# Reordering the start-up tiles of a cross-attention and spectral-FFN kernel: transposes, evictions and norms trade places in five tiles

## The chip, the cores and the metric

The kernel runs on one core of one Trainium2 chip. A core has a matrix engine (TensorE, "PE" in the profile, with weight loads shown apart as "PEld"), a vector engine (VectorE, "DVE"), an activation engine (ScalarE, "ACT"), a general engine (GpSimd, "POOL") and a queue that issues DMAs (SyncE, "SP"). Each engine works through its own list of instructions in order. The metric is device time in microseconds, the median of several runs; lower is better.

## What is computed

Everything is float32. `x` is (2, 2048, 512), the context is (2, 128, 512), 16 heads of 32.

```python
def attention(x, enc, mask):            # x already layer-normed
    q, k, v = x @ wq + bq, enc @ wk + bk, enc @ wv + bv      # split into 16 heads
    score = (q @ k.T) / sqrt(32) * mask
    score = where(score == 0, -1e9, score)
    return softmax(score) @ v @ wo + bo

def ffn(x):                             # x already layer-normed
    y_freq = fft(x) @ (w_real + 1j * w_imag)
    return real(ifft(y_freq)) + bias

x = x + attention(layernorm(x), ctx, mask)
x = x + ffn(layernorm(x))
```

The FFN is linear, so the kernel folds both transforms and the complex weight into one real 512 x 512 matrix, `m_ffn`, computed once on the chip.

## The kernel before

**Tiling.** The 4096 rows are taken in 8 groups of 512 rows (`i`), each of 4 row tiles of 128 (`t`). A tile is written here as (group, row tile). A group goes through these stages: its rows less their first element (`relative`, on POOL for most groups), row statistics on DVE, `query_norm` on DVE, `query_transposes` (four 128x128 transposes on PE and a copy by ACT into `xnT`), four query chains `q[0]` to `q[3]` (PE, evicted by ACT with the bias), then for each row tile scores and softmax, the transposes of the weights, `context`, the output projection `o[t]`, a second layer norm, and the FFN chain `y`.

**One tile of the softmax.** `begin(i, t)` issues 32 score matmuls into two PSUM tiles, a half of 8 heads each. For each half: `masked` (DVE, L345, PSUM to SBUF), `maxima` (DVE: L352 over the whole half, the reduction L354, and the tiny L355), `exponentials` (ACT: eight L361 activations, each with a read of its accumulator), `divided` (a reciprocal on DVE, L373, and the product on POOL, L374). Then `transposed_weights(i, t, first, end, eng)`: for each of four head sets, four transposes on PE (L391) into a PSUM bank and a copy out by ACT (L398), or by DVE (L396) where `nc.vector` is given. Both halves must have been divided before any of it.

**Buffers.** PSUM has two buffers of each kind: `sc` for scores (two banks each), `tp` for transposes, `mm` for chains. The third user of a `tp` or `mm` buffer waits until the copy or eviction of the first is done. In SBUF, `rel` has 4 buffers, `xnT` and `cT` one, `w` (a half of the weights) five.

**What runs beside the first tiles.** In tiles (0,1) to (1,1) the start-up work is woven in: the second value chain `values[1]`; the matrix `m_ffn`, made from four `First` products `h[0]` to `h[3]` (PE, evicted by ACT; `first()` is four small POOL operations, L676 and L678; `second()` two DVE operations, L689 and L690) and four `Mirrored` products `m[0]` to `m[3]` (PE, evicted by two ACT operations, L731 and L737, then two POOL operations, L738 and L739); the queries of groups 1 and 2; the statistics and norms of groups 2 and 3. Each `Mirrored` product reads all four halves that `second()` finishes. `load_first_rows` sends four small DMAs on SP's queue that read the result of `h[2]`.

**Order.** The order of instructions is written out by hand: every engine runs its share of the calls in the order in which the Python code makes them, and semaphores are set from the buffers read and written. For (0,0) to (1,0) the calls stand one by one; from (1,1) on a helper, `slot(...)`, issues a tile from lists of work. Its argument `soon=True`, used for (1,1), puts the exponentials ahead of the first chain's eviction, and the second half's exponentials ahead of the second pair of weight transposes.

The few lines that show what a chain with work in between does:

```python
for c in range(NC):
    nc.tensor.matmul(ps, lhs(c), rhs(c), start=(c == 0), stop=(c == NC - 1))
    if c == HC - 1:
        call(between)
```

Of the kernel before, what the change touches and what calls it, by code (L numbers as in the profile page):

```python
# [22 lines left out]
def kernel(  # L23
# [34 lines left out]
    nc = tc.nc  # L58
# [5 lines left out]
    NC = D // P  # L64
    NR = P // DH
    HH = H // 2
    TG = 4
# [6 lines left out]
    work = ctx.enter_context(tc.tile_pool(name="work", bufs=2))  # L74
# [11 lines left out]
    HC = NC // 2  # L86
# [36 lines left out]
    def load_residual(i):  # L123
        b, q0 = place(i)
        xs = groups[i] = big_tile("x", 2, f"x_{i}")
        for t in range(TG):
            nc.sync.dma_start(xs[:, t, :], x[b, q0 + t * P : q0 + (t + 1) * P, :])
# [146 lines left out]
    def query_norm(i, t):  # L274
        mv, rstd = stats[i]
        normalize(rels[i][t], rels[i][t], mv[:, t, :], rstd[:, t : t + 1])

    def query_transposes(i, t):
        if t == 0:
            xnTs[i] = big_tile("xnT", 1, f"xnT_{i}")  # L280
        transpose_rows(
            xnTs[i][:, :, t * P : (t + 1) * P], rels[i][t], f"a{i}_{t}", nc.scalar
        )

    class Queries:
# [5 lines left out]
        def pe(self):  # L291
            i, g = self.i, self.g
            if i not in qTs:
                qTs[i] = big_tile("qT", 2, f"qT_{i}")
            self.ps = chain(
                f"q_{i}_{g}",
                lambda c: wq[:, c, g * P : (g + 1) * P],
                lambda c: xnTs[i][:, c, self.first * P :],
                width=GQ - self.first * P,
                spare=self.spare,  # L300
            )
# [78 lines left out]
    def transposed_weights(i, t, first, end, eng=None, banks=None):  # L380
        if t == 0 and first == 0:
            pts[i] = [big_tile("pt", 6, f"pt_{i}_{g}") for g in range(NC)]
        ws = weights[i, t]
        for g in range(first, end):
            ps = (
                banks[g]
                if banks
                else ps_tp.tile([P, NR, P], FP, tag="tp", name=f"tpw_{i}_{t}_{g}")
            )
            for r in range(NR):  # L390
                nc.tensor.transpose(  # L391
                    ps[:, r, :], ws[r // 2].w[:, (r % 2) * NC + g, :], ident
                )
            dst = pts[i][g][:, :, t * P : (t + 1) * P]
            if eng:
                eng.tensor_copy(dst, ps)  # L396
            else:
                nc.scalar.copy(dst, ps)  # L398
# [4 lines left out]
    def context(i, first, end, eng=nc.scalar):  # L403

        b = place(i)[0]
        if first == 0:
            cTs[i] = big_tile("cT", 1, f"cT_{i}")
        cT = cTs[i]
        for g in range(first, end):
            ps = ps_mm.tile([P, GQ], FP, tag="mm", name=f"c_{i}_{g}")  # L410
            for r in range(NR):
                h = g * NR + r
                nc.tensor.matmul(  # L413
                    ps[r * DH : (r + 1) * DH, :],
                    v[:, b, h * DH : (h + 1) * DH],
                    pts[i][g][:, r, :],
                    start=True,
                    stop=True,
                )
            if eng is nc.scalar:  # L420
                nc.scalar.copy(cT[:, g, :], ps)
            else:
                eng.tensor_copy(cT[:, g, :], ps)

    def output_bias(i):

        xs = groups[i]
        for t in range(TG):
            nc.gpsimd.tensor_tensor(xs[:, t, :], xs[:, t, :], bo, ALU.add)  # L429
# [153 lines left out]
    class Values:  # L583
        def __init__(self, b):
            self.b = b

        def pe(self):
            self.ps = chain(
                f"v_{self.b}",
                lambda c: encT[:, c, self.b * K : (self.b + 1) * K],  # L590
                lambda c: wv[:, c, :],
            )

        def evict(self):
# [148 lines left out]
    def run(job):  # L743
        job.pe()
        job.evict()

    def begin(i, t):
        sc = scores(i, t)
        weights[i, t] = [Softmax(i, t, hf, sc[hf]) for hf in range(2)]
        return weights[i, t]  # L750
# [110 lines left out]
    h = [First(what, g) for what in range(2) for g in range(HC)]  # L861
    m = [Mirrored(f"m_{g}", half_of(g), m_ffn[:, g, :]) for g in range(NC)]
    rest = [Queries(0, g, 1, g >= HC) for g in range(NC)]
    q = [Queries(1, g) for g in range(NC)]
    values = [Values(b) for b in range(B)]

    w = begin(0, 0)
# [21 lines left out]

    w = begin(0, 1)  # L890
    w[0].masked()
    for t in range(TG):
        query_transposes(1, t)
        relative(2, t, nc.gpsimd)
    w[0].maxima()
    values[1].pe()
    w[0].exponentials()
    w[1].masked()
    values[1].evict()
# [3 lines left out]
    w[1].exponentials()  # L903
    h[0].evict()
    w[0].divided()
    transposed_weights(0, 0, HC, NC, nc.vector)
    query_statistics(2, 0, TG)
    run(q[0])
    w[1].divided()
    h[0].first()  # L910

    load_rows(3)
    w = begin(0, 2)
    w[0].masked()
    q[1].pe()
    w[0].maxima()
    w[0].exponentials()
    w[1].masked()
    q[1].evict()
    transposed_weights(0, 1, 0, HC, nc.vector)  # L920
    w[1].maxima()
    run(q[2])
# [2 lines left out]
    for t in range(TG):  # L925
        query_norm(2, t)
    w[0].divided()
    h[0].second()
    run(q[3])
    w[1].divided()  # L930

    q = [Queries(2, g) for g in range(NC)]
    w = begin(0, 3)
    w[0].masked()
    h[1].pe()
    h[1].evict()
    h[1].first()
    w[0].maxima()
    h[2].pe()
    h[2].evict()  # L940
    h[2].first()
    w[0].exponentials()
    w[1].masked()
    transposed_weights(0, 2, 0, HC, nc.vector)
    h[1].second()
    h[3].pe()
    h[3].evict()
    h[3].first()
    for t in range(TG):
        query_transposes(2, t)  # L950
    w[1].maxima()
    w[0].divided()
    relative(3, 0, nc.gpsimd)
# [2 lines left out]
    load_residual(0)  # L956
    rows_m = load_first_rows("rows_m", [x.lhs(HC)[0:1, :] for x in m])
    w[1].exponentials()
    transposed_weights(0, 2, HC, NC, nc.vector)
    run(q[0])  # L960
    w[1].divided()
    relative(3, 1, nc.gpsimd)

# [1 line left out]
    w = begin(1, 0)  # L965
    w[0].masked()
    m[0].pe()
    add = first_rows("add_m", rows_m)
# [2 lines left out]
    relative(3, 2, nc.gpsimd)  # L971
    relative(3, 3, nc.gpsimd)
    m[1].pe()
    w[0].exponentials()
    w[1].masked()
    transposed_weights(0, 3, 0, HC, nc.vector)
    w[1].maxima()
    w[0].divided()
    m[1].evict(add[:, 1:2])
    m[2].pe()  # L980
    m[2].evict(add[:, 2:3])
    transposed_weights(0, 3, HC, NC)
# [5 lines left out]
    w[1].divided()  # L988
    query_statistics(3, 2, TG)

    def last_of_m():
        m[3].pe()
        m[3].evict(add[:, 3:4])


    for i in range(1, last - 1):
        p, pp, n, nn = i - 1, i - 2, i + 1, i + 2
        q = [Queries(n, g) for g in range(NC)]
        q_nn = Queries(nn, 0)
        o = [Project(p, t) for t in range(TG)]  # L1000
        f_p = Ffn(p, 0)
        second = [q[2], q[3], None]
        if i > 1:
            f_pp = [Ffn(pp, t) for t in range(TG)]
            second = [q[2], q[3], f_pp[3]]

        def if_pp(*work):
            return list(work) if i > 1 else []

        if i > 1:  # L1010
            load_rows(nn)
            load_mask(n)
            load_residual(p)
            slot(
                i,
                0,
                [f_pp[1], f_pp[2], q[1]],
                turned=(p, TG - 1),
                early=[(ffn_transposes, pp, 2)],
                pool=[(relative, nn, t, nc.gpsimd) for t in range(TG)],  # L1020
                on_b=[(ffn_norm, pp, 3), (query_statistics, nn, 0, 2)],
                on_c=[(query_statistics, nn, 2, TG)],
                end=[(context, p, 0, 2)],
            )
        slot(
            i,
            1,
            second,
            turned=(i, 0),
            soon=(i == 1),  # L1030
            early=[
                (context, p, 2, NC),
                (ffn_transposes, pp, 3) if i > 1 else (last_of_m,),
            ],
            pool=[(output_bias, p)],
            on_b=[(query_norm, nn, 0), (query_norm, nn, 1)],
        )
        slot(
            i,
            2,  # L1040
            o[:3],
            turned=(i, 1),
            early=[(query_transposes, nn, 0), (query_transposes, nn, 1)],
            on_a=[(ffn_statistics, p, 0)],
            on_b=[(ffn_norm, p, 0), (query_norm, nn, 2), (query_norm, nn, 3)],
            on_c=[(ffn_statistics, p, 1)],
            end=[(ffn_transposes, p, 0)],
        )
        slot(
            i,  # L1050
            3,
            [o[3], f_p, q_nn],
            turned=(i, 2),
            early=[(query_transposes, nn, 2), (query_transposes, nn, 3)],
            on_a=[(ffn_statistics, p, 2)],
            on_b=[(ffn_norm, p, 1), (ffn_statistics, p, 3)],
            on_c=[(ffn_norm, p, 2)],
            end=[(ffn_transposes, p, 1)],
        )
# [4 lines left out]
    i, n, p, pp = last - 1, last, last - 2, last - 3  # L1064
    load_mask(n)
    load_residual(p)
    q = [Queries(n, g) for g in range(NC)]
# [7 lines left out]
        turned=(p, TG - 1),  # L1075
# [184 lines left out]
```

## Time and profile before

| | us |
|---|---|
| median of 3 runs | 539.77 (538.93 to 540.01) |
| profiled execution | 538.45 |
| its span, first to last instruction | 536.4 |
| PE busy in the span | 524.0 |
| DVE busy | 446.2 |
| ACT busy | 336.4 |
| POOL busy | 336.8 |

PE works at its full granted clock throughout. The span is the time from the first to the last instruction on the core; 2.05 us of the execution lie around it. Busy shares are averages over the whole span; the tiles that the change touches lie between about 36 and 111 us. The scores of the tiles begin on PE at these times:

| tile | (0,1) | (0,2) | (0,3) | (1,0) | (1,1) | (1,2) | (1,3) |
|---|---|---|---|---|---|---|---|
| scores start, us | 35.95 | 50.68 | 64.95 | 81.34 | 96.64 | 110.14 | 127.22 |

### The profile page before, as it was taken

What the parts mean: (1) busy time and instruction counts of PE and PEld (TensorE: products, weight loads), DVE (VectorE), ACT (ScalarE), POOL (GpSimd) and SP (SyncE); (2) the same over time, 40 slices, a digit from 0 to 9 for tenths busy, and PEclk for the clock granted to TensorE, in tenths of its full rate; (3) what the DMA queues carried; (4) which work ended last, traced back from release to release, by engine and by line L of the source; (5) the groups of instructions that cost most, each with busy time, mean ns of one, the idle gap of its engine ahead of it and who ended that gap; (6) DMA issues with size and microseconds to landing.
All of it is one profiled execution on the core that took longest, in us unless ns stands there. A gap on an engine that the chain in (4) does not pass through costs nothing.

```text
span 536.4 us, 8808 instructions
## 1 busy us (share of the span) xinstructions
PE 524.0 (98%) x3028; PEld 293.8 (55%) x3028; DVE 446.2 (83%) x623; ACT 336.4 (63%) x1284; POOL 336.8 (63%) x276
## 2 busy tenths in 40 slices
PE   8999989989999999999999999999999999999997
PEld 7755576445545555455545555455545555455444
DVE  4789999899887998879987999879967899899351
ACT  3376676566687666666777666666777676766210
POOL 2769487935795449825795459925755466856450
PEclk9999999999999999999999999999999999999999
DMA  9962020000510006000510005000310201301102
GB/s 318 384 221 78 1 81 20 1 1 0 185 53 2 20 24 208 7 20 1 186 51 0 21 14 203 20 21 0 117 43 25 75 0 60 100 0 41 39 0 79
DMA packets 22892, 36.49 MB, mean 68 GB/s; under 512 B 2104, under 2 KB 7488, under 8 KB 22848
## 3 DMA queue, kind: packets, MB, share of 16 engines
q1 hardware_dynamic: 22160, 34.75, 18.8%
q10 hardware_dynamic: 688, 1.18, 0.6%
q8 instruction: 24, 0.39, 0.3%
q14 instruction: 20, 0.16, 0.1%
HBM read 27.53 MB, written 8.39 MB: 67 GB/s over the span
## 4 chain that ended last, share of the span: by engine, by line
PE 73%; DVE 19%; ACT 6%; DMA 1%; issue 1%; SPq 0%; ACTq 0%; DVEq 0%
PE y L210 16%; PE o L210 16%; PE q L210 15%; PE tpw L391 7%; PE c L413 5%; PE sc L326 5%; ACT w L361 5%; DVE w L352 5%; DVE nmax L354 4%; DVE w L345 4%; PE tp_a L194 2%; PE tp_f L194 2%; PE k L558 1%; DVE nmax L355 1%; DVE norm_f L227 1%; DMA enc<-in_ctx_dram 1%
## 5 line engine op out<-in xcount | busy, mean ns | idle before, releaser
L361 ACT ACTIVATE w<-w,nmax 128x128 f32<-128x128 f32 x512 | 198.3, 395 | 26.7 <-DVE nmax L355 26.0
L374 POOL TENSOR_TENSOR w<-w,rden 128x1024 f32<-128x1024 f32 x62 | 118.2, 1907 | 79.8 <-DVE rden L373 62.2
L210 PE MATMUL o<-wo,cT 128*128 128x512 f32 x256 | 115.3, 594 | 0.0
L210 PE MATMUL q<-xnT,wq 128*128 128x512 f32 (+1 forms) x256 | 111.8, 581 | 1.5 <-ACT odd_m L737 0.9
L210 PE MATMUL y<-m_ffn,nT 128*128 128x512 f32 x248 | 112.1, 594 | 0.5 <-DVE x L514 0.5
L361 ACT ACTIVATION_READ_ACCUMULATOR w<-w,nmax 128x1 f32 x512 | 99.3, 194 | 0.0
L398 ACT COPY pt<-tpw 128x512 f32<-128x512 f32 x110 | 58.8, 586 | 56.8 <-PE tpw L391 56.6
L352 DVE SCALAR_TENSOR_TENSOR w<-w 128x1024 f32<-128x1024 f32 x64 | 89.9, 1405 | 0.8
L345 DVE TENSOR_TENSOR w<-sc,mask 128x1024 f32<-128x1024 f32 x64 | 77.4, 1211 | 13.2 <-PE sc L326 12.5
L354 DVE TENSOR_REDUCE nmax<-w 128x8 f32<-128x1024 f32 x64 | 78.1, 1220 | 2.2
L391 PEld LDWEIGHTS tpw<-ident,w 128*128 128x128 f32 x496 | 57.5, 141 | 31.9 <-issue 28.3
L210 PEld LDWEIGHTS o<-wo,cT 128*128 128x128 f32 x256 | 46.2, 190 | 47.5 <-issue 46.1
L210 PEld LDWEIGHTS q<-xnT,wq 128*128 128x128 f32 x256 | 46.4, 190 | 46.6 <-issue 40.2
L210 PEld LDWEIGHTS y<-m_ffn,nT 128*128 128x128 f32 x248 | 44.5, 190 | 45.2 <-issue 44.2
L391 PE MATMUL tpw<-ident,w 128*128 128x128 f32 x496 | 65.2, 274 | 0.8 <-ACT pt L398 0.4
L469 POOL TENSOR_TENSOR x<-x,bf 128x512 f32<-128x512 f32 x32 | 50.4, 1576 | 19.1 <-DVE norm_f L227 19.1
L223 POOL TENSOR_SCALAR rstd_f<-mv_f 128x1 f32<-128x1 f32 x32 | 17.9, 558 | 65.3 <-DVE mv_f L220 65.3
L429 POOL TENSOR_TENSOR x<-x,bo 128x512 f32<-128x512 f32 x32 | 48.1, 1532 | 0.0
L244 POOL TENSOR_SCALAR rel<-rows 128x512 f32<-128x512 f32 x26 | 43.6, 1689 | 1.6 <-PE tp_a L194 1.6
L326 PEld LDWEIGHTS sc<-kT,qT 32*128 32x128 f32 x1024 | 31.4, 186 | 15.3 <-issue 13.6
L196 ACT COPY nT<-tp_f 128x512 f32<-128x512 f32 x29 | 16.9, 583 | 34.1 <-PE tp_f L194 34.0
L373 DVE RECIPROCAL rden<-den 128x8 f32<-128x8 f32 x64 | 12.6, 197 | 30.9 <-ACT w L361 30.8
(92 smaller groups left out, 566.1 us busy)
## 6 DMA issues: line engine op xcount, KB each, us to landing
rows<-in_x_dram SPq DMA_DIRECT2D x32, 256.0 KB, 4.2
x<-in_x_dram SPq DMA_DIRECT2D x32, 256.0 KB, 4.5
out_dram<-x SPq DMA_DIRECT2D x31, 256.0 KB, 2.0
mask<-in_mask_Bx1xSxS_fk_dram SPq DMA_DIRECT2D x8, 256.0 KB, 4.7
wk<-in_L_xattn_wk_w_dram ACTq DMA_DIRECT2D x2, 512.0 KB, 7.0
wq<-in_L_xattn_wq_w_dram SPq DMA_DIRECT2D x1, 1024.0 KB, 6.8
wr<-n_L_ffn_w_freq_real_dram SPq DMA_DIRECT2D x2, 512.0 KB
wi<-n_L_ffn_w_freq_imag_dram SPq DMA_DIRECT2D x2, 512.0 KB, 8.2
```

What stands on the lines that cost most here:

```text
L210: nc.tensor.matmul(ps, lhs(c), rhs(c), start=(c == 0), stop=(c == NC - 1))
L244: eng.tensor_scalar(d, xt, xt[:, 0:1], None, ALU.subtract)
L326: nc.tensor.matmul(sc[r // 2][:, r % 2, g, :], qTs[i][rows, g, t * P : (t + 1) * P], kT[rows, g, b * K : (b + 1) * K], start=True, stop=True,)
L345: nc.vector.tensor_tensor(self.w, self.sc.rearrange("p r g k -> p (r g) k"), self.mrow, ALU.mult)
L352: nc.vector.scalar_tensor_tensor(w, w, 0.0, w, ALU.is_equal, ALU.subtract)
L354: nc.vector.tensor_reduce(self.nmax, w, AX.X, ALU.min)
L361: nc.scalar.activation(w[:, h, :], w[:, h, :], AF.Exp, bias=self.nmax[:, h : h + 1], scale=-UNIT, accum_out=self.den[:, h : h + 1],)
L374: eng.tensor_tensor(w, w, rden.unsqueeze(2).to_broadcast([P, HH, K]), ALU.mult)
L391: nc.tensor.transpose(ps[:, r, :], ws[r // 2].w[:, (r % 2) * NC + g, :], ident)
L398: nc.scalar.copy(dst, ps)
L429: nc.gpsimd.tensor_tensor(xs[:, t, :], xs[:, t, :], bo, ALU.add)
L469: nc.gpsimd.tensor_tensor(xt, xt, bf, ALU.add)
```

## The change

Nothing is added or taken out of the computation; calls trade places, and one group of copies changes its engine.

- Tile (0,1): two of the four transposes of group 1's rows stay behind the scores; the other two go into the middle of the second value chain. The chain `q[0]` goes ahead of the second pair of weight transposes, whose copies move from DVE to ACT.
- Tile (0,2): `q[1]` is evicted ahead of the exponentials; `h[0].second()` moves out to the next tile.
- Tile (0,3): the transposes of group 2's rows go right behind the scores, two ahead of `h[1]` and two behind it; `h[2]` and `h[3]` go behind the first exponentials; `h[0].second()` comes in; `q[0]` goes ahead of the second pair of weight transposes.
- Tile (1,0): `m[1]` is evicted ahead of the exponentials.
- Tile (1,1) is written out rather than issued by `slot`: the second pair of weight transposes, with its copies, goes ahead of the second half's exponentials; two norms of group 3 go ahead of the division of the first half; `output_bias` goes behind `m[3]`'s eviction.

```diff
-        def pe(self):
+        def pe(self, between=()):
             self.ps = chain(
                 f"v_{self.b}",
                 lambda c: encT[:, c, self.b * K : (self.b + 1) * K],
                 lambda c: wv[:, c, :],
+                between=between,
             )
...
 
     w = begin(0, 1)
     w[0].masked()
+    query_transposes(1, 0)
+    query_transposes(1, 1)
     for t in range(TG):
-        query_transposes(1, t)
         relative(2, t, nc.gpsimd)
     w[0].maxima()
-    values[1].pe()
+    values[1].pe(between=[(query_transposes, 1, 2), (query_transposes, 1, 3)])
     w[0].exponentials()
     w[1].masked()
     values[1].evict()
...
     w[1].exponentials()
     h[0].evict()
     w[0].divided()
-    transposed_weights(0, 0, HC, NC, nc.vector)
+    q[0].pe()
+    transposed_weights(0, 0, HC, NC)
+    q[0].evict()
     query_statistics(2, 0, TG)
-    run(q[0])
     w[1].divided()
     h[0].first()
 
     load_rows(3)
     w = begin(0, 2)
     w[0].masked()
-    q[1].pe()
+    run(q[1])
     w[0].maxima()
     w[0].exponentials()
     w[1].masked()
-    q[1].evict()
     transposed_weights(0, 1, 0, HC, nc.vector)
     w[1].maxima()
     run(q[2])
...
     for t in range(TG):
         query_norm(2, t)
     w[0].divided()
-    h[0].second()
     run(q[3])
     w[1].divided()
 
     q = [Queries(2, g) for g in range(NC)]
     w = begin(0, 3)
     w[0].masked()
+    query_transposes(2, 0)
+    query_transposes(2, 1)
     h[1].pe()
+    query_transposes(2, 2)
+    query_transposes(2, 3)
     h[1].evict()
+    w[0].maxima()
+    h[0].second()
     h[1].first()
-    w[0].maxima()
-    h[2].pe()
-    h[2].evict()
-    h[2].first()
     w[0].exponentials()
     w[1].masked()
     transposed_weights(0, 2, 0, HC, nc.vector)
     h[1].second()
+    h[2].pe()
+    h[2].evict()
+    h[2].first()
     h[3].pe()
     h[3].evict()
     h[3].first()
-    for t in range(TG):
-        query_transposes(2, t)
     w[1].maxima()
     w[0].divided()
     relative(3, 0, nc.gpsimd)
...
     load_residual(0)
     rows_m = load_first_rows("rows_m", [x.lhs(HC)[0:1, :] for x in m])
     w[1].exponentials()
+    run(q[0])
     transposed_weights(0, 2, HC, NC, nc.vector)
-    run(q[0])
     w[1].divided()
     relative(3, 1, nc.gpsimd)
 
...
     relative(3, 2, nc.gpsimd)
     relative(3, 3, nc.gpsimd)
     m[1].pe()
+    m[1].evict(add[:, 1:2])
     w[0].exponentials()
     w[1].masked()
     transposed_weights(0, 3, 0, HC, nc.vector)
     w[1].maxima()
     w[0].divided()
-    m[1].evict(add[:, 1:2])
     m[2].pe()
     m[2].evict(add[:, 2:3])
     transposed_weights(0, 3, HC, NC)
...
     w[1].divided()
     query_statistics(3, 2, TG)
 
-    def last_of_m():
-        m[3].pe()
-        m[3].evict(add[:, 3:4])
+    w = begin(1, 1)
+    w[0].masked()
+    context(0, 2, NC)
+    m[3].pe()
+    m[3].evict(add[:, 3:4])
+    output_bias(0)
+    w[0].maxima()
+    q[2].pe()
+    w[0].exponentials()
+    w[1].masked()
+    q[2].evict()
+    transposed_weights(1, 0, 0, HC, nc.vector)
+    w[1].maxima()
+    run(q[3])
+    transposed_weights(1, 0, HC, NC)
+    w[1].exponentials()
+    query_norm(3, 0)
+    query_norm(3, 1)
+    w[0].divided()
+    w[1].divided()
 
 
     for i in range(1, last - 1):
...
         q_nn = Queries(nn, 0)
         o = [Project(p, t) for t in range(TG)]
         f_p = Ffn(p, 0)
-        second = [q[2], q[3], None]
-        if i > 1:
-            f_pp = [Ffn(pp, t) for t in range(TG)]
-            second = [q[2], q[3], f_pp[3]]
-
-        def if_pp(*work):
-            return list(work) if i > 1 else []
-
         if i > 1:
             load_rows(nn)
             load_mask(n)
             load_residual(p)
+            f_pp = [Ffn(pp, t) for t in range(TG)]
             slot(
                 i,
                 0,
...
                 on_c=[(query_statistics, nn, 2, TG)],
                 end=[(context, p, 0, 2)],
             )
-        slot(
-            i,
-            1,
-            second,
-            turned=(i, 0),
-            soon=(i == 1),
-            early=[
-                (context, p, 2, NC),
-                (ffn_transposes, pp, 3) if i > 1 else (last_of_m,),
-            ],
-            pool=[(output_bias, p)],
-            on_b=[(query_norm, nn, 0), (query_norm, nn, 1)],
-        )
+            slot(
+                i,
+                1,
+                [q[2], q[3], f_pp[3]],
+                turned=(i, 0),
+                early=[(context, p, 2, NC), (ffn_transposes, pp, 3)],
+                pool=[(output_bias, p)],
+                on_b=[(query_norm, nn, 0), (query_norm, nn, 1)],
+            )
         slot(
             i,
             2,
```

## The prediction

> **What bounds the kernel now.** I read the page first: the engine shares, then windows of TensorE (PE), then PE's waits, then the chain of waits, and last the timeline of VectorE (DVE) and GpSimd (POOL) where two operations stretch each other.
>
> ```profile
> PE 524.0 (98%) x3028; PEld 293.8 (55%) x3028; DVE 446.2 (83%) x623; ACT 336.4 (63%) x1284; POOL 336.8 (63%) x276
> ```
>
> PE carries the span, so a reordering can only win where PE stands still. The windows (start:end, length, PE busy) say where that is:
>
> ```profile
> 36.00:113.70 77.70, 71.56 (x507) 1.00 0.10 32
> 113.70:128.30 14.60, 14.60 (x84) 1.00 0.00 1
> 128.30:142.90 14.60, 14.60 (x88) 1.00 0.23 69
> ```
>
> From 36 to 113.7 us, the very tiles that are edited, PE is idle for 77.70 - 71.56 = 6.1 us; after that it is full. The waits of PE up to 120 us (total, times, longest):
>
> ```profile
> PE tp_a L194 <- ACT pt L398: 2.3, 1, 2.3
> PE tp_a L194 <- ACT xnT L196: 1.7, 3, 1.2
> ...
> PE q L210 <- ACT odd_m L737: 0.9, 1, 0.9
> PE q L210 <- ACT qT L307: 0.7, 1, 0.7
> PE tpw L391 <- ACT pt L398: 0.4, 1, 0.4
> ```
>
> All end on a copy or eviction by ScalarE (ACT). Why ACT is late is in the chain of waits:
>
> ```profile
> 87.24 3.19 ACT w L361 x16
> 90.43 0.36 ACT m_ffn L731
> 90.79 0.26 ACT odd_m L737
> 91.06 0.04 issue
> 91.10 3.70 PE q L210 x8
> ...
> 111.41 1.73 ACT w L361 x9
> 113.14 0.48 ACT pt L398
> 113.61 0.04 issue
> 113.66 1.14 PE tp_a L194 x8
> ```
>
> PE's next work needs a PSUM buffer whose copy is queued behind eight exponentials. But between such places the same chain runs through DVE (masked product, L352, L354) for most of 36 to 91 us: PE's gaps are partly the echo of a slow DVE, and this decides how much of the 6.1 us comes back. DVE itself is slowed by POOL, as the timeline shows:
>
> ```profile
> 52.92 1.90 POOL L374 TENSOR_TENSOR w<-w,rden 128x1024 f32<-128x1024 f32 x1
> 53.15 2.75 DVE L352 SCALAR_TENSOR_TENSOR w<-w 128x1024 f32<-128x1024 f32 x1
> ...
> 77.16 1.90 POOL L374 TENSOR_TENSOR w<-w,rden 128x1024 f32<-128x1024 f32 x1 [0.27 <-DVE rden L373]
> 77.22 2.12 DVE L690 TENSOR_TENSOR half<-u_half 128x254 f32<-128x254 f32 x1
> ```
>
> L352 takes 1.22 us alone and 2.75 beside a division; L690 0.4 alone and 2.12.
>
> **What the Trainium skill says.** "SBUF — State Buffer", section "Who interferes with whom": DVE and GpSimd share one port pair under an exclusive lock; a DVE operation with two SBUF inputs, or a tensor_scalar in a 2-port mode, and a GpSimd operation shut each other out for the whole instruction, whoever starts first. The trace agrees: L352 ended 1.1 us after the division's end (55.90 against 54.82); copies out of PSUM and the reductions (1.22 us throughout) aren't touched. "Perfetto Trace Analysis", section "Identifying the Most-Contended Engine", warns that matmul busy time is a poor measure of distance to the peak. I use it only to find idle PE, where it serves: the gaps have named waits.
>
> **The change part by part.** I follow PE, ACT, DVE and POOL by hand with the durations of the timeline: scores 1.10, two sets of transposes 0.87, a chain 3.44, a First 1.95, a Mirrored 1.93 (PE, start to start); masked product 1.25, L352 1.22, L354 1.25, two PSUM copies 1.27, a norm 0.45 (DVE); eight exponentials 3.1, an eviction 0.68, two copies 1.05 (ACT); a division 1.90 (POOL). A tile is (group, row tile).
>
> S1, tile (0,1). Before, transposes and value chain take PE from 37.05 to 42.86 = 5.81. With two transposes inside the chain it is 0.87 + 3.44 + 0.87 = 5.2. With q[0] put before the second pair of weight transposes their 0.4 wait is covered: 42.2 + 0.87 + 1.95 + 3.44 + 0.87 gives scores of (0,2) at 49.4 (was 50.68). DVE loses two copies to ACT, 1.27, but the fourth row statistic now waits for POOL's relative at 49.8; the masked product of (0,2) starts at 50.8 (was 51.89). POOL's relatives need the two later transposes read first; these are done by 40.5, before subtract_columns frees POOL at 42.5: nothing.
>
> S2, tile (0,2). The weight transposes of (0,1) need its second division, and POOL is full from 39.42 to 54.8 (subtract, relatives, division, rstd), so that doesn't move, 54.8 to 55.2: PE, early at 53.95, idles 1.25 and q[2] starts at 56.1 as before (56.20). The early part is given back here. Then q[1] evicted ahead of the exponentials removes 0.7 to 0.8 before q[3]; scores of (0,3) at 64.0 (was 64.95). h[0].second leaves DVE's queue between norms and second reciprocal, where the division stretched it to 2.4: the masked product of (0,3) starts at 65.1 (was 66.61).
>
> S3, tile (0,3). Transposes behind the scores and around h[1] take out PE waits of 1.2 + 0.2 + 0.2 and the gap before them; scores of (1,0) could start at 79.0 (was 81.34). Against it, ACT's new order is xnT copies, h[1].evict, exponentials (70.0, was 71.31), and only then h[2].evict (73.1, was 70.21) and h[3].evict (73.7, was 74.40). POOL's h[2].first waits for L352's port until 74.4; h[2].first and h[3].first take 1.65 each, and with h[2].second between them h[3].first ends at 78.2 (was 76.89). Then h[3].second on DVE and the first division on POOL both want the port. No row of before shows who wins from this start. DVE first: h[3].second ends at 79.1. POOL first: 78.2 + 1.9 + 0.8 to 1.1 = 81.2; was 80.41. m[0] reads every half row and waits for it, and two DVE copies, the reciprocal and the masked product of (1,0) stand behind: that product at 80.4 or 82.5 (was 82.55). I take the middle and keep both ends. The row loads on SP's queue stand behind h[2].second (77.6, was 79.34), not behind h[3].
>
> S4, tile (1,0). m[1].evict ahead of the exponentials frees the buffer for q[1]: the 0.9 wait goes. Exponentials start between 84.9 and 87.3 (was 87.24), q[1] between 88.5 and 90.2 (was 91.10), scores of (1,1) between 93.8 and 95.6 (was 96.64): 1.0 to 2.8 gained, middle 1.9. On POOL the two m[1] operations (1.5) go ahead of a division whose reader runs after 102 us: hidden by about 6 us.
>
> S5, tile (1,1) and the next. Copies ahead of the second exponentials take away the 2.3 wait of tp_a, and norms ahead of the division cost 0.9 in place of 2.53. PE's scores of (1,2) come at 110.14 - 1.9 = 108.2 and the transposes follow with no wait. But the second exponentials now wait for the last weight copy: they start 1.05 later relative to PE, at 109.1 (was 109.96), end at 112.2, and behind their reciprocal stands the masked product of (1,2): 112.35 (was 113.29), 0.95 earlier only. The division ends at 114.2, and PE, with o[0] done at 113.2, waits 1.0 for it; then norm_f of (0,0), 125.6 before, ends at 124.65, and PE, there at 122.85, waits 1.8. So 126.69 becomes 124.65: 2.0. The 2.3 is mostly replaced by waits on DVE's chain. output_bias behind m[3] on POOL ends near 107, read at 118: nothing; with that cover gone it would cost its 1.5.
>
> **Sum.** After 128 us PE was full, and the work is the same, so 2.0 stays: span 536.4 - 2.0 = 534.4, execution 538.45 - 2.0 = 536.4. The median of the runs, 539.77, stands 1.3 above the profiled execution; I take the difference over to it: 537.8.
>
> **Rivals.** 0.2% of 539.77 is 1.08 us; below that this measurement can't tell a change.
> (a) The forecast: waits of ACT go, DVE's chain takes their place, 1.1 to 2.9 gained, 537.8. Chance 0.45.
> (b) DVE wins the port in S3 and the stretched L352 shrink as well: PE recovers 3 to 4.5 of its 6.1, about 536.2. For it: h[0].second, norms and two copies leave DVE, 1.7 + 1.6 + 1.3 = 4.6 of its time. Against it: POOL's queue is full to 54.8 and again near 80 to 99. Chance 0.23.
> (c) The waits come back entirely: POOL wins in S3 and the 1.05 of S5 counts in full: 0 to 1 gained, 539.3. Chance 0.20.
> (d) Slower: POOL becomes the bound in tile (0,3). If h[2].first and h[3].first, now behind the exponentials, end 1 us later than my 78.2, and L689 loses the port to the division and L690 to the relative (1.6 more), h[3].second ends at 83.8; every us beyond 81.2 takes one from the 1.1 of its end: -1.5, 541.3. It decides from h[3].second ending at 82.3 (slower at all) or 83.4 (measurably). Chance 0.12.
>
> **Range.** 535.6 to 540.1: (a) and (c) whole and half of (b). Faster by over 0.2% 0.68, within 0.2% 0.20, slower 0.12.
>
> **What would show it.** Right: the 2.3, 0.9 and 0.7 waits are gone; tp_a of group 3 follows the scores of (1,2) directly; new PE waits on POOL w L374 and on norm_f appear near 54, 113 and 123; the h[3].second pair ends between 79 and 81.3; PE's scores of (1,3) start near 125.2 (was 127.22). Wrong: no new PE wait at tiles (0,2) and (1,2), or idle PE of over 6 us before 127. The forecast falls if h[3].second ends after 82, or if PE's windows after 128 are no longer full.

## The result and the profile after

| | before | changed |
|---|---|---|
| median, us | 539.89 (4 runs) | 535.32 (4 runs: 534.98 to 536.54) |
| ratio, 95% interval | | 0.9922 (0.9901 to 0.9943) |
| profiled execution, us | 538.45 | 534.98 |
| its span, us | 536.4 | 533.0 |
| the same on another chip, median, us | 538.18 (11 runs) | 534.63 (6 runs) |
| ratio there, 95% interval | | 0.9943 (0.9928 to 0.9958) |

By the medians the change makes the kernel faster by 0.6 to 0.8%; the profiled executions differ by 3.5 us and their spans by 3.4. The kernel before takes one of two values some 1.6 us apart, 536.4 to 537.0 or 537.9 to 539.9 on the later chips: all 37 executions of the lower kind had a granted clock of at least 0.999, but 30 of the 45 of the upper kind had one of 0.996 or 0.997, so that in these the clock may be the cause (0.3% of the 524.0 us that PE is busy would be 1.6 us, by estimate). The profiled execution shown ahead of the prediction is one of the upper kind, at full clock; the last section comes back to it. Between the lower values of the two kernels on the second chip, 536.8 to 536.9 and 534.2 to 534.7, the gain is 2.2 us, or 0.4%.

In the changed kernel the new code shifts later lines by one (L657 becomes L658, L690 and L691 are the two operations of `second()`). The windows of PE that answer to those shown of before (start:end, length, PE busy, instructions, granted clock, DMA share, GB/s):

```profile
36.00:113.70 77.70, 75.06 (x526) 1.00 0.10 32
113.70:128.30 14.60, 12.93 (x76) 1.00 0.00 1
128.30:142.90 14.60, 14.60 (x82) 1.00 0.42 134
```

Up to 113.7 us PE is idle for 2.6 us in place of 6.1; but the next window, full before, now has a gap of 1.7. The waits of PE from 0 to 120 us, and those after 120 us:

```profile
PE tpw L391 <- DVE pt L396: 1.4, 1, 1.4
...
PE tpw L391 <- POOL w L374: 0.9, 2, 0.5
PE tpw L391 <- ACT xnT L196: 0.3, 1, 0.3
...
PE tp_a L194 <- ACT xnT L196: 0.2, 1, 0.2
```

```profile
PE tp_f L194 <- DVE norm_f L227: 1.9, 2, 1.7
```

The 2.3, 1.7, 0.9 and 0.7 us on ACT are gone or down to 0.5 together. In their place stand waits on DVE and POOL: copies in (1,0), the divisions of (0,1) and (1,1), and `norm_f` in (1,2).

Starts of the score matmuls on PE show where the 3.4 us came from. The third row is a second profile of the kernel before, of its lower value (536.88 us, span 534.9), the fourth one of the changed kernel on that chip (span 532.5).

| tile | (0,1) | (0,2) | (0,3) | (1,0) | (1,1) | (1,2) | (1,3) | (0,1) to (1,3) |
|---|---|---|---|---|---|---|---|---|
| before | 35.95 | 50.68 | 64.95 | 81.34 | 96.64 | 110.14 | 127.22 | 91.27 |
| changed | 35.58 | 49.09 | 63.14 | 77.49 | 93.19 | 106.70 | 123.84 | 88.26 |
| before, again | 35.05 | 49.12 | 63.40 | 79.85 | 95.15 | 108.65 | 125.72 | 90.67 |
| changed, again | 35.07 | 48.58 | 62.62 | 76.98 | 92.68 | 106.19 | 123.33 | 88.26 |

I call the last column the stretch; it is the measure of the experiments, since it leaves out most of the start-up's DMAs. It is read from one profile of each kernel; the changed kernel gave 88.26 on both chips. Between the two first rows it shrinks by 3.01; 0.37 more lie ahead of (0,1), before any edit. Of the 3.01, 1.83 are idle time of PE (6.14 us of the stretch before, 4.31 after). The other 1.18 are busy time, 85.13 and 83.95 us for the same 559 instructions: not all of the gain stood in the profile as a wait. After (1,3) nothing differs: 536.4 - 127.22 = 409.18 and 533.0 - 123.84 = 409.16. Between the last two rows it shrinks by 2.41, tile by tile: 0.56 in (0,1), 0.24 in (0,2), 2.09 in (0,3), then -0.40, -0.01 and -0.07. Tile (1,1), with the largest wait of the kernel before, gives nothing in the end. That asked for experiments.

### The profile page after: what moved, and what is told of

Read it like the earlier page. It is cut to its first block, busy times and chain, and to the rows that moved or that the text cites. A ratio compares the mean times of both kernels' runs of the same rounds, so it can differ in the third digit from the quotient of the medians.

```text
span 533.0 us, 8813 instructions
## 1 busy us (share of the span) xinstructions
PE 522.4 (98%) x3028; PEld 293.3 (55%) x3028; DVE 440.6 (83%) x621; ACT 337.5 (63%) x1286; POOL 336.8 (63%) x276
## 3 DMA queue, kind: packets, MB, share of 16 engines
q10 hardware_dynamic: 688, 1.18, 0.6%
## 4 chain that ended last, share of the span: by engine, by line
PE 74%; DVE 17%; ACT 4%; issue 2%; POOL 1%; DMA 1%; SPq 0%; ACTq 0%; POOLq 0%; DVEq 0%
PE y L210 16%; PE q L210 16%; PE o L210 14%; PE tpw L391 7%; PE c L413 5%; PE sc L326 5%; DVE w L352 4%; ACT w L361 3%; DVE nmax L354 3%; DVE w L345 3%; PE tp_f L194 2%; PE tp_a L194 2%; PE k L558 1%; DVE norm_f L227 1%; PE v L210 1%
## 5 line engine op out<-in xcount | busy, mean ns | idle before, releaser
L374 POOL TENSOR_TENSOR w<-w,rden 128x1024 f32<-128x1024 f32 x62 | 119.3, 1924 | 74.1 <-DVE rden L373 56.6
L352 DVE SCALAR_TENSOR_TENSOR w<-w 128x1024 f32<-128x1024 f32 x64 | 88.1, 1377 | 0.8
L244 POOL TENSOR_SCALAR rel<-rows 128x512 f32<-128x512 f32 x26 | 44.7, 1731 | 1.3 <-PE tp_a L194 1.3
```

The costliest lines, as they stand in the source:

```text
L244: eng.tensor_scalar(d, xt, xt[:, 0:1], None, ALU.subtract)
L352: nc.vector.scalar_tensor_tensor(w, w, 0.0, w, ALU.is_equal, ALU.subtract)
L374: eng.tensor_tensor(w, w, rden.unsqueeze(2).to_broadcast([P, HH, K]), ALU.mult)
```

## The experiments

Theory T is that of the prediction: DVE's chain, slowed by POOL on their shared port, sets PE's pace, and a wait of PE on ACT is worth only what DVE leaves of it. Rival R: each wait on ACT that goes is worth its length. All times below stand beside the kernel before on the same chip, whose median was 536.95 for the first four experiments, 538.26 for the next four and 538.18 for the last. Medians of the kernel before move with the mix of its two values, so I judge by the stretch and give the times beside it.

**Tile (1,1) alone, both ways.** First the changed kernel with its (1,1) in the old order:

```diff
     w[0].masked()
+    output_bias(0)
     context(0, 2, NC)
...
-    output_bias(0)
...
     run(q[3])
-    transposed_weights(1, 0, HC, NC)
     w[1].exponentials()
+    transposed_weights(1, 0, HC, NC)
+    w[0].divided()
     query_norm(3, 0)
     query_norm(3, 1)
-    w[0].divided()
     w[1].divided()
```

> The changed kernel with tile (1,1) in its old order. Measure: the stretch on PE from the first score matmul of (0,1) to that of (1,3), 91.27 us before, 88.26 changed. Theory T (PE's gaps after the edit are set by DVE's chain): the 2.3 us wait of tp_a on ACT's copies comes back, and the new waits on norm_f (1.67) and on the division (0.44) vanish for it; stretch 88.3, within 0.6, time within 0.1% of the changed kernel. Rival R (each wait on ACT is worth its length): stretch 90.6, time 2.3 us above the changed kernel.

Measured: stretch 88.18, against 88.26; median 534.62 us, ratio to before 0.9946 (0.993 to 0.9963). Then the kernel before with the new (1,1) alone (the same lines, the other way):

> The kernel before with tile (1,1) alone in the new order. T: the 2.3 us wait of tp_a goes and is replaced by waits on norm_f and on the division; stretch 91.3, within 0.6, time within 0.1% of before. R: stretch 89.0, time 2.3 us below before.

Measured: stretch 90.71, against 90.67; median 537.03 us, ratio 0.999 (0.9979 to 1.0001). The waits of PE from 100 to 127 us, of the changed kernel with the old (1,1) and then of the kernel before with the new one:

```profile
PE tp_a L194 <- ACT pt L398: 2.3, 1, 2.3
```

```profile
PE tp_f L194 <- DVE norm_f L227: 1.7, 1, 1.7
PE tpw L391 <- POOL w L374: 0.4, 1, 0.4
```

The two are exchanged for each other to within 0.2 us. R is out for the largest of the waits: its 2.3 us were worth nothing here. The chain of waits of the changed kernel has the way from one to the other:

```profile
106.98 0.60 ACT pt L398
107.59 3.08 ACT w L361 x16
110.67 0.02 issue
110.69 0.20 DVE rden L373
110.89 1.10 DVE w L345
111.99 0.02 issue
112.02 2.01 DVE w L352
...
121.37 1.77 DVE norm_f L227
123.14 0.14 issue
123.28 0.63 PE tp_f L194 x4
```

The copies ahead of the exponentials free PE's buffer and delay the exponentials; the reciprocal waits for them, and the masked product of the next tile stands behind it on DVE, and everything of that tile up to `norm_f`.

**`h[0].second()` back in (0,2).**

```diff
     w[0].divided()
+    h[0].second()
     run(q[3])
...
     w[0].maxima()
-    h[0].second()
     h[1].first()
```

> The changed kernel with h[0].second() back in tile (0,2), behind the reciprocal of the first half. T: L691 stands beside the division on the shared port again, 2.1 us in place of 0.4, the masked product of (0,3) starts about 1.5 later and all of DVE's chain with it; stretch 89.5 (88.9 to 89.9), time 1.2 us above the changed kernel. R: no wait of PE on ACT returns, stretch 88.3.

Measured: stretch 88.35, median 534.63 us, ratio 0.9944 (0.9922 to 0.9966). T's number fell, and R's 88.3 stood. L691 did take 2.12 us beside the division, but DVE would have stood still there anyway: in the changed kernel it waits 2.29 us until 63.69 for the exponentials. The move is worth 0.1 at most. This execution had L352 of (0,0) behind POOL (last section) and lost 0.3 in (0,2); the variant with copies on DVE, below, ran into the same and lost 0.43 there without this edit.

**Tile (0,1) back.**

```diff
-    query_transposes(1, 0)
-    query_transposes(1, 1)
     for t in range(TG):
+        query_transposes(1, t)
         relative(2, t, nc.gpsimd)
...
-    values[1].pe(between=[(query_transposes, 1, 2), (query_transposes, 1, 3)])
+    values[1].pe()
...
-    q[0].pe()
-    transposed_weights(0, 0, HC, NC)
-    q[0].evict()
+    transposed_weights(0, 0, HC, NC, nc.vector)
     query_statistics(2, 0, TG)
+    run(q[0])
```

> The changed kernel with tile (0,1) in its old order. T: PE reaches the weight transposes of (0,1) 1.3 us later, but these wait for POOL's division in both orders; q[2] starts at the same place, stretch 88.3, within 0.4. R: PE's 1.3 is lost, stretch 89.6, time 1.3 us above the changed kernel.

Measured: stretch 89.68, 1.42 more; median 535.98 us, ratio 0.9973 (0.9963 to 0.9984). R's number, but not R's way: PE reaches the scores of (0,3) even earlier here, 27.42 after those of (0,1) against 27.56, and loses the time in (0,3) and (1,0). The timeline of (0,2) shows why, first of the changed kernel, then of this one (start, length):

```profile
51.55 1.23 DVE L352 SCALAR_TENSOR_TENSOR w<-w 128x1024 f32<-128x1024 f32 x1
51.65 2.89 POOL L374 TENSOR_TENSOR w<-w,rden 128x1024 f32<-128x1024 f32 x1
```

```profile
51.32 1.90 POOL L374 TENSOR_TENSOR w<-w,rden 128x1024 f32<-128x1024 f32 x1
51.56 2.74 DVE L352 SCALAR_TENSOR_TENSOR w<-w 128x1024 f32<-128x1024 f32 x1
```

In the changed order DVE takes the port 0.1 us ahead of POOL, and the division pays (2.89); in the old order POOL is 0.24 ahead and L352 pays (2.74), which is the row of the kernel before as well. The order of (0,1) goes with this every time: in all ten profiles with the new (0,1) L352 takes 1.22 to 1.27 us there, in all four with the old one 2.74 or 2.75.

The 1.5 us don't go straight down DVE's chain. At the masked product of (0,3) only 0.40 is left (29.16 after the scores of (0,1) against 28.76), since DVE waits 1.40 for the exponentials in place of 2.29. But POOL's divisions came later with DVE, the second one ends 1.2 later, and L352 of (0,3) stands behind it for longer, 2.25 us in place of 1.42. At the second masked product of (0,3) DVE is 1.45 late. The trial turns back all of tile (0,1), with the engine of its copies, so the tie isn't isolated as the cause.

**The transposes of group 2 back behind `h[3]`.**

```diff
-    query_transposes(2, 0)
-    query_transposes(2, 1)
     h[1].pe()
-    query_transposes(2, 2)
-    query_transposes(2, 3)
...
     h[3].first()
+    for t in range(TG):
+        query_transposes(2, t)
     w[1].maxima()
```

> The changed kernel with the four transposes of group 2's rows back behind h[3] in tile (0,3). T: PE reaches the scores of (1,0) about 1.9 us later (near 79.4 in place of 77.49), with its wait on ACT xnT again, but the masked product of (1,0) on DVE stands behind h[3].second() and two copies until 80.3 in both; stretch from the scores of (0,1) to those of (1,3) 88.3 (88.0 to 88.7). R (waits on ACT are worth their length): stretch 90.0, time 1.6 us above the changed kernel.

Measured: stretch 88.72; median 535.04 us, ratio 0.9952 (0.9938 to 0.9966). This is 0.02 above T's range, and R's 90.0 is out. PE has its waits on ACT xnT back, 1.09 and 0.69, and its scores of (1,0) come 44.14 after those of (0,1) in place of 41.91: 2.2 later. Of these, 0.46 are left at (1,3). So these transposes make up most of the 2.09 that (0,3) shows in the table, and most of what they win there is lost again by (1,3).

**`m[1]`'s eviction back behind the exponentials of (1,0).**

```diff
     m[1].pe()
-    m[1].evict(add[:, 1:2])
     w[0].exponentials()
...
     w[0].divided()
+    m[1].evict(add[:, 1:2])
     m[2].pe()
```

> The changed kernel with m[1].evict() back behind the exponentials of (1,0). T: q[1] waits for m[1]'s buffer until about 88.8 in place of 87.76, DVE's eviction of q[1] and all behind it wait for PE: stretch 89.2 (88.9 to 89.5), time 0.9 us above the changed kernel. Rival: the wait on DVE's copies (1.38) hides it, stretch 88.4.

Measured: stretch 89.38, 1.12 more; median 535.7 us, ratio 0.997 (0.9958 to 0.9982). This lies in T's range. The wait on ACT odd_m is 0.86 again, and DVE, which evicts `q[1]`, now waits for it, as it doesn't in the changed kernel:

```profile
91.81 0.75 DVE L309 TENSOR_SCALAR qT<-q,bq 128x512 f32<-128x512 f32 x1 [1.04 <-PE q L210]
```

This wait is worth its length because here PE is on DVE's chain.

**Two edits that attack what is left.** One puts the copies of (1,1) on DVE, so that the exponentials need not wait:

```diff
-    transposed_weights(1, 0, HC, NC)
     w[1].exponentials()
     query_norm(3, 0)
     query_norm(3, 1)
     w[0].divided()
+    transposed_weights(1, 0, HC, NC, nc.vector)
     w[1].divided()
```

> The changed kernel with tile (1,1) in a third order: the second half's exponentials directly behind q[3]'s eviction, then norms and the first division, then the second pair of weight transposes with their copies on DVE. T: exponentials start 1.05 earlier, so the reciprocal, the masked product of (1,2) and norm_f come 1.0 to 1.2 earlier; PE waits up to 1.0 for DVE's copies ahead of tp_a, and no longer for norm_f; stretch 87.1 (86.8 to 87.5), time 1.1 us below the changed kernel. Rival: the copies on DVE cost 1.3 there and nothing is won, stretch 88.3 or more.

Measured: stretch 88.00; median 534.17 us, ratio 0.9923 (0.9896 to 0.9949). The wait on `norm_f` shrinks to 0.91 and PE waits 0.51 for the copies. From the scores of (1,2) to those of (1,3) it takes 16.46 in place of 17.14, 0.68 less, where T had 1.0 to 1.2; another 0.43 was lost in (0,2), in an execution that again had L352 of (0,0) behind POOL. T's range (86.8 to 87.5) is missed, and so is the rival's 88.3 or more.

The other lets `h[3].second()` run ahead of the division in (0,3):

```diff
     w[1].maxima()
-    w[0].divided()
-    relative(3, 0, nc.gpsimd)
     h[2].second()
     h[3].second()
+    w[0].divided()
+    relative(3, 0, nc.gpsimd)
```

> The changed kernel with h[2].second() and h[3].second() ahead of the first half's reciprocal and division in tile (0,3), so that the division can't take the port between h[3]'s two operations. T: L691 of h[3] takes 0.4 in place of 2.12, the masked product of (1,0) comes 1.3 earlier, PE's wait of 1.38 on DVE's copies shrinks; stretch 87.6 (87.2 to 87.9), time 0.7 us below the changed kernel. Rival: the division, 0.7 later, holds up POOL's queue and the weight transposes of (0,3) as much: stretch 88.3.

Measured: stretch 87.46, 0.80 less; median 533.45 us (4 runs), ratio 0.9919 (0.9887 to 0.9951). The timeline of DVE, first of the changed kernel, then of this one:

```profile
76.92 2.12 DVE L691 TENSOR_TENSOR half<-u_half 128x254 f32<-128x254 f32 x1
78.96 1.28 DVE L396 COPY pt<-tpw 128x512 f32<-128x512 f32 x2
...
80.27 1.17 DVE L345 TENSOR_TENSOR w<-sc,mask 128x1024 f32<-128x1024 f32 x1
```

```profile
76.54 0.42 DVE L691 TENSOR_TENSOR half<-u_half 128x254 f32<-128x254 f32 x1
...
76.98 1.24 DVE L396 COPY pt<-tpw 128x512 f32<-128x512 f32 x2
...
78.25 1.22 DVE L345 TENSOR_TENSOR w<-sc,mask 128x1024 f32<-128x1024 f32 x1
```

L691 takes 0.42 in place of 2.12, and the masked product of (1,0) comes 1.6 earlier (counted from the scores of (0,1), 43.12 against 44.69). PE's wait on DVE's copies (1.38) is gone. T's range holds. Its advantage over the changed kernel, 0.8 us, is clear in the stretch, not in the intervals of the times; its profiled execution, 533.55 us, is the shortest of all kernels here, by 0.04.

Both edits together:

> The changed kernel with both edits: copies on DVE in (1,1) and h[2].second(), h[3].second() ahead of the division in (0,3). T: their gains stand on different parts of DVE's chain and add up, 0.8 and 0.7: stretch 86.8 (86.5 to 87.2), time 1.4 us below the changed kernel. Rival: PE is the bound after the first of them; stretch 87.4.

Measured: stretch 87.49, median 534.45 us (6 runs), ratio 0.994 (0.9923 to 0.9957). They don't add: with PE earlier at (1,1), the transposes wait 1.74 us for the copies on DVE. This is the rival's number, but not its reason: PE isn't the bound, it waits for DVE's copies, and that wait takes the gain.

**`h[2]` back ahead of the exponentials of (0,3).**

```diff
     h[1].first()
+    h[2].pe()
+    h[2].evict()
+    h[2].first()
     w[0].exponentials()
...
     h[1].second()
-    h[2].pe()
-    h[2].evict()
-    h[2].first()
     h[3].pe()
```

> The changed kernel with h[2] (product, eviction, first()) back ahead of the exponentials of (0,3). T: exponentials start 1.2 later, which nothing on DVE's chain waits for, and POOL's six small operations of h[2] and h[3] end earlier; h[3].second() ends 0.5 to 2 earlier, stretch 87.5 (86.2 to 88.2). Rival (ACT's exponentials are the bound there): stretch 89.4.

Measured: stretch 89.91, median 534.81 us, ratio 0.995 (0.9932 to 0.9969). The profiled execution took 536.42 and its other runs 534.7 to 534.9; it lost 1.4 in (0,2), where POOL's L224 and the division came behind L352 and PE waited 1.50, which the edit doesn't touch (last section). From the scores of (0,3) to those of (1,3) it takes 60.98, the changed kernel 60.70. So nothing is won: T's 0.5 to 2 fell, because the division now stood beside the L691 of `h[2]` (2.11) and PE waited 1.28 for the DMAs of rows_m. R's 1.1 later isn't there either.

**The ten trials together.** T's range held in four of them ((1,1) both ways, `m[1]`, `h[3].second()`) and was missed by 0.02 in one; in the other five its number fell. Of the three waits on ACT that were put back, 2.3, 1.8 and 0.86 us, only the last was worth its length. So R is refuted as a rule, and of T the direction is shown; where DVE stands still anyway, and which way the port falls, it did not foresee.

**Both kernels again, on one chip.**

> The changed kernel again, beside the kernel before on this chip. T: the kernel before has two values, 536.9 and 538.4, by who takes the shared port in tile (0,0), POOL's cols<-wi or DVE's L352, a matter of when the DMA of wi lands; the changed kernel takes 534.5 to 535.1 in both cases, since its tiles (0,1) and (0,2) have slack for it. Ratio 0.995. Rival: the changed kernel has the same two values 1.5 us apart, ratio 0.994 to 0.996 too, but with values near 536.3.

> The kernel before, profiled again. T: where L352 of tile (0,0) takes 1.2 us (DVE first), the execution takes 536.9 and the stretch is 90.6; where it takes 2.9 (POOL first), 538.4 and 91.3. Rival: no relation between the two.

Measured: the kernel before 536.88 us, L352 of (0,0) 1.22 us, stretch 90.67, as T had it. The changed kernel's six runs: 534.16 to 534.65 and one of 536.15, ratio 0.9943 (0.9928 to 0.9958). T had the changed kernel free of a second value, at 534.5 to 535.1 us; the one at 536.15 lies near the 536.3 of the rival, so T fell here. No profile of such an execution was kept.

## Why the prediction was right, and where it wasn't

**The bound and the mechanism.** Right in the main. The gain lies in the start-up, where PE had its gaps, and everything after (1,3) stayed as it was (409.18 and 409.16 us). But the prediction counted idle time of PE alone, and that is 1.83 of the 3.01 us of the stretch. The waits on ACT went, and waits on POOL w L374 near 54 and 113 and on `norm_f` near 123 took their place, at 54.59, 112.99 and 123.28.

**S1, tile (0,1).** PE's way to the scores of (0,2) was 13.51 us against a worked 13.45. What the prediction took from it, nothing beyond (0,2), was wrong: it held that POOL's division gives the early part back. On PE it does; but the masked product, which comes 14.71 us after the scores of (0,1) in place of 15.28 with the tile's old order, lets DVE take the port before that division, and the trial puts 1.42 us on the whole tile.

**S2, tile (0,2).** PE's idle was worked out at 1.25 and was 0.48 by the wait. That the division of (0,1) "doesn't move" came true by luck: counted from the scores of (0,1) it ended at 18.96 (before 18.87), but POOL came to it 0.90 earlier, and then it took 2.89 in place of 1.90 behind L352. The term for `h[0].second()`, 1.5 us on DVE, was mis-sized: 0.1, as DVE waits for the exponentials in the same place.

**S3, tile (0,3).** Who would win the port was left open between 79.1 and 81.2 for the end of `h[3].second()`. POOL won, as L691's 2.12 shows, and yet it ended at 79.04, because `h[3].first()` ended at 76.70 and not at 78.2: `h[2]` was evicted at 72.2 in place of 73.1, and L352 gave the port back early enough for `h[2].first()` to start at 72.9 in place of 74.4. This is the largest mis-sized term, 1.5 us. What the lost port costs was measured by winning it: 0.8 us in the stretch.

**S4.** The scores of (1,1) were worked out 1.0 to 2.8 earlier, and came 3.45 earlier, 0.37 of it from ahead of (0,1). `m[1]`'s eviction, put at 0.9, is worth 1.12.

**S5.** Right in its balance, and the sharpest of them: the tile was said to return most of what it takes, and taking it out or adding it alone moves the stretch by -0.08 and 0.04. Of its parts, the wait on the division, put at 1.0, was 0.44, and that on `norm_f`, put at 1.8, was 1.67.

**The sum.** 2.0 us were forecast on the profiled execution's own time. It was 3.4 in the span, of which 0.37 lies ahead of any edit. Of the 3.0 left, 0.6 belongs to the upper value of the kernel before; beside its lower value the change brings 2.41. The rest of the 4.57 between the medians is the step from the profiled execution to the median: the prediction carried the 1.3 us over to the changed kernel. The median of the kernel before lies 1.44 above its profiled execution, that of the changed kernel 0.34 above; no run here shows why. The measured ratio, 0.9922, makes 535.6 of 539.77, at the lower end of the range, and the changed kernel's own median, 535.32, lies below it. So the mechanism was forecast better than the size: 2.0 us against 4.2 by the ratio, or against 2.41 between like profiles. By the medians rival (b) came nearest: L352 shrank in (0,2) as it said, but DVE did not win the port in (0,3). The 2.41 lie in the 1.1 to 2.9 of (a).

What stays open: `q[1]`'s earlier eviction in (0,2) and `q[0]` ahead of the weight transposes in (0,3) were not tried alone. Put back one by one, the parts that were tried are worth 1.42 ((0,1)), 1.12 (`m[1]`), 0.46 (the transposes of group 2), 0.09 (`h[0].second()`) and -0.08 us ((1,1)). That is 3.0 together, more than the 2.41, so they aren't independent.

## What to carry to other kernels

The length of a wait isn't its worth. A wait of 2.3 us went and was worth nothing, one of 0.9 us was worth 1.1; the difference was whether the engine behind PE's next wait was moved too, which one can read ahead of time by following the late engine's queue to the next place where PE needs it. Where two engines share a port, look for pairs that start within a few tenths of a microsecond of each other, and put the one that is needed later behind the other by the order of the code rather than leave it to chance: one such pair was worth 0.8 us here.

## What the runs showed of the hardware

In the kernel before, a tie on the port that DVE and GpSimd share falls either way. In tile (0,0), which the change doesn't touch, POOL's `cols<-wi` starts when a DMA lands, and L352 comes within about half a microsecond of it. The timeline of the first profile of the kernel before (538.45 us), and of the second (536.88 us):

```profile
22.88 2.35 POOL L620 TENSOR_TENSOR cols<-wi 128x1020 f32<-128x1020 f32 x1 [1.23 <-DMA wi<-n_L_ffn_w_freq_imag_dram]
23.36 2.94 DVE L352 SCALAR_TENSOR_TENSOR w<-w 128x1024 f32<-128x1024 f32 x1
```

```profile
22.46 1.22 DVE L352 SCALAR_TENSOR_TENSOR w<-w 128x1024 f32<-128x1024 f32 x1
22.98 2.91 POOL L620 TENSOR_TENSOR cols<-wi 128x1020 f32<-128x1020 f32 x1 [1.48 <-DMA wi<-n_L_ffn_w_freq_imag_dram]
```

Whoever starts second is stretched, here by 1.7 us if it is DVE (L352, 2.94 against 1.22) and by 0.6 if it is POOL. That is the whole-instruction lock of the Trainium skill's "SBUF — State Buffer", "Who interferes with whom"; what I hadn't expected is that a lead of 0.1 us (51.55 against 51.65 in (0,2)) decides over 1.5 us of L352's time.

The two executions differ by 1.57 us, but the tie isn't all of that: 0.90 was there when the scores of (0,0) started, at 20.90 us in the first and 20.00 in the second. The DMA landed at nearly the same time in both, so it was DVE's later start that brought L352 behind POOL. In the stretch the two differ by 0.60. One profile of each kind shows that the tie goes with the value, not that it is the whole cause.

Three of the variants of the changed kernel were profiled with POOL first in (0,0): `h[0].second()` back 534.98 us, copies on DVE 534.15, `h[2]` ahead, with its loss in (0,2), 536.42. So the changed order can absorb most of that cost, but not always. What parts them is a second tie, in (0,2), between L352 and POOL's small L224, which stands ahead of the division. First of the variant with `h[0].second()` back, where L352 starts at 51.62, then of that with `h[2]` ahead, where it starts at 51.66:

```profile
51.61 1.04 POOL L224 TENSOR_TENSOR rstd<-rstd,power 128x4 f32<-128x4 f32 x1
```

```profile
51.66 2.13 POOL L224 TENSOR_TENSOR rstd<-rstd,power 128x4 f32<-128x4 f32 x1
```

In the second L224 lost, the division behind it ended at 55.65 us in place of 54.64, and PE waited 1.50 for it. That the changed kernel's own high values, 536.15 and 536.54, come from this tie is likely, but not shown.

The hold is not equally long for all of POOL's work. In the kernel before, L352 at 89.45 took 1.21 us, unhindered, while POOL's one-input L244 ran from 88.7 to 90.3, and behind the L224 that started 0.01 ahead of it (51.61) it took only 1.27. The page has the second wait for the whole instruction; in these two places the measurement says otherwise. Beside a 128x1024 division that had started first, L352 was held up in every place shown here.
